# A conv-attention hybrid on one core: a warm start from one half with ten steps, new orders of issue, and the last group of a recurrence stored plainly

## Chip, core and metric

The kernel runs on one core of one Trainium2 chip. The metric is the device time of one execution in microseconds, the median of several runs. The profile is of one further execution. The engines are called as in the profile: PE is TensorE's matmuls, PEld its weight loads, DVE VectorE, ACT ScalarE, POOL GpSimd, SP SyncE.

## What is computed

The input is x of 4 x 128 x 64 x 64 (batch, channels, rows, columns), in fp32. Layer 0 is a layer norm over channels, a depthwise 3x3 convolution added to it, and attention inside 16 x 16 windows with a 5 x 5 neighbourhood (two branches, four heads), added to x. Layer 1 works on the 4096 tokens of each image: a causal linear attention, and then a feed-forward part that ends in a serial recurrence:

```python
t = t + _L1_attn_ref(_ln_t(t), L1_attn_W, L1_attn_b)      # elu features, cumulative sums
t = t + _L1_ffn_ref(_ln_t(t), L1_ffn_W, L1_ffn_V, L1_ffn_gamma, L1_ffn_beta)

# inside _L1_ffn_ref: Wx is batch-normed over all 4 x 4096 tokens
def step(yt, wx_t):
    yt = jax.nn.sigmoid(wx_t + yt @ Vt)
    return (yt, yt)
y0 = jnp.zeros((B, H), dtype=Wx.dtype)
_, ys = jax.lax.scan(step, y0, jnp.swapaxes(Wx, 0, 1))
```

V is orthogonal and the sigmoid's slope is at most a quarter, so the recurrence forgets its start quickly.

## The kernel before

**Main stage.** The 64 rows of an image are cut into four bands of 16, a band into four windows; there are 16 bands and 64 windows. For each band `front()` yields layer norm and convolution in small pieces (`norm_rows`, `convolve`, L314-418: measure, scale, turn, then nine taps, the first on ScalarE, eight on VectorE at L378). For each window `block()` does q, k, v (L427, L440), logits and their exponentials (L480, L489), `sums` (L509, the denominators, copied to `den` and sent by DMA to `dc`), `values` (L524), `inverse` (L535 and L537 on VectorE, then a DMA to `rd` and one from there into `rden`) and `scaled` (L552, on POOL, into oT). When the four windows of a band have their oT, layer 1 does the band in two halves, called a and c (or y and z when the next band is already there): output (L578, 585), measure, norm, turn, queries, keys, values, turn_keys, scores, accumulate, attend0, attend1, measure_last, keep, send, spread, product. product (L726) multiplies by W of the feed-forward part into `wx` and takes the batch norm's statistics of it. send and spread carry the layer norm's factors through DRAM (L609, L620), so that product needs no turned copy; the very last half has none and goes through norm_last and turn_last instead (L730, 731).

**What sets the order.** All engines work in the order of the program; `in_order()` fixes it. The order is written out by hand: `SLOT` is that of a window in the loop, with six gaps (0 to 5); `LAYER1` fills the 24 gaps of a band's four windows with layer 1's operations, `AHEAD` with pieces of `front()`. `START` is the order of everything before the loop's first window (window 4), `TAIL` that of everything after the logits of window 63. `prepare` (L201) folds weights together once. `mul.2` and `mul.3` do the convolution of windows 2 and 3 of the first band on TensorE (nine taps of two matmuls each, four taps at the first call and five at the second, L396); `conv.0` and `conv.1` do windows 0 and 1 on VectorE. `warm.n` asks for n filler matmuls (L259) before the next matmul group; they compute nothing that is used.

**Recurrence.** An image's 4096 steps are cut into 128 segments of 32, run side by side: 512 columns in three groups (L931). Every segment is first run for WARM = 11 steps from zero over the last 11 steps of its segment; the end state is handed to the next segment as its start (L1007), and then 32 counted rounds run. In each round TensorE adds V·y to seeded sums (L1004; VectorE writes the seeds of two rounds at a time, L942) and ScalarE takes the sigmoid (L1009). Outputs of images 0 and 1: four rounds fill a buffer `ys` (three of them), and a DMA on POOL's queue adds it to what `keep` put into the output before (L1016, accumulating). Outputs of images 2 and 3: the residual was parked by `keep`, is loaded into `res` (L913), and POOL adds it round by round into `ot` (L1022), which SP sends (L1028). At the end VectorE compares the 32nd state of every segment with the handed state (L1035), within 5e-7; if any differs by more, `general()` computes everything again with the plain serial recurrence.

Of the kernel before, what the change touches and what calls it, by code (L numbers as in the profile page):

```python
# [9 lines left out]
F32 = mybir.dt.float32  # L10
# [7 lines left out]
P = 128  # L18
# [20 lines left out]
WARM = 11  # L39
# [4 lines left out]
    "measure_last.z",  # L44
# [3 lines left out]
    "norm.a",  # L48
    "measure.c keep.z",
    "",  # L50
    "turn.a norm.c",
    "",
    "",
    "keys.a product.z",
    "turn.c queries.a",
    "values.a",
    "turn_keys.a scores.a keys.c",
    "accumulate.a values.c",
    "turn_keys.c attend0.a queries.c",
    "attend1.a",  # L60
    "scores.c",
    "measure_last.a",
    "accumulate.c keep.a send.a",
# [3 lines left out]
    "",  # L67
)
SLOT = ("sums", "values", "logits", 0, "scaled", "inverse", 1, "q", 2, 3, "k", "v", 4, 5)
AHEAD = ("03", "01223345", "001245", "00234")  # L70
START = (
    "warm.5 conv.0 prepare q.0 front conv.1 mul.2 mul.3",
    "mul.2 k.0 front v.0 q.1 k.1 logits.0 front",
    "q.2 front front front front mul.3 v.1 front",
    "logits.1 sums.0 k.2 values.0 v.2 front front front",
    "inverse.0 front front load.2 front logits.2 q.3 front",
    "front sums.1 scaled.0 front values.1 inverse.1 q.4 k.4",
    "sums.2 k.3 front front front v.3 scaled.1 logits.3",
    "values.2 v.4 inverse.2 front front",
)  # L80
TAIL = (
    "scaled.61 keep.w output.y send.w sums.63 spread.w output.z measure.z",
    "measure.y inverse.62 norm.z values.63 product.w norm.y turn.y scaled.62",
    "keys.y queries.y scores.y turn_keys.y inverse.63 turn.z values.z values.y",
    "queries.z keys.z accumulate.y warm.1 attend0.y turn_keys.z product.v attend1.y",
    "measure_last.y scores.z accumulate.z send.y spread.y attend0.z attend1.z keep.y",
    "measure_last.z warm.2 send.z scaled.63 product.y warm.10 output.a measure.a",
    "output.c measure.c norm.a spread.z keep.z turn.a norm.c turn.c",
    "queries.a queries.c keys.a values.a keys.c turn_keys.a values.c scores.a",
    "accumulate.a attend0.a attend1.a scores.c turn_keys.c measure_last.a accumulate.c keep.a",  # L90
    "attend0.c send.a attend1.c measure_last.c spread.a keep.c norm_last.c product.a",
    "turn_last.c product.z product.c",
# [20 lines left out]
def conv_attn_hybrid(ctx: ExitStack, tc: tile.TileContext, ins: dict, out: bass.AP):  # L113
# [120 lines left out]
    wx = const.tile([P, B, NH, SEG, HSEGS], F32, name="wx")  # L234

# [490 lines left out]
    def product(h):  # L726

        wps = bank()
        if h.factors is None:
            nc.tensor.matmul(wps, fwT, h.xl, start=True, stop=True)  # L730
            nc.scalar.copy(wx[:, h.b, h.hb], wps.rearrange("p (k s) -> p s k", s=SEG))
        else:
            nc.tensor.matmul(wps, fwT, h.rs.rearrange("p s k -> p (s k)"), start=True, stop=True)  # L733
            nc.vector.tensor_tensor(
                wx[:, h.b, h.hb].rearrange("p s (j a) -> p s j a", a=P // SEG),
                wps.rearrange("p (s j a) -> p s j a", j=4, a=P // SEG),
                h.factors.rearrange("p (a s) j -> p s j a", s=SEG),
                ALU.mult,
            )
# [147 lines left out]
    which.update(a=Half(len(bands) - 1, 0), c=Half(len(bands) - 1, 1))  # L887
    for what in " ".join(TAIL).split():
        if what.partition(".")[2].isdigit():
            block(what)  # L890
        else:
            do(what, which)
# [11 lines left out]
    ring = rec.enter_context(tc.tile_pool(name="ring", bufs=3))  # L904
# [4 lines left out]
    res = sp.tile([P, B // 2, NH, SEG, HSEGS], F32, name="res")  # L909
    for s0 in (0, SEG // 2):  # L910
        steps_of, cols = slice(s0, s0 + SEG // 2), slice(s0 * HSEGS, (s0 + SEG // 2) * HSEGS)
        for i, b in enumerate(resd):
            (nc.sync, nc.scalar)[i].dma_start(  # L913
                res[:, i, :, steps_of].rearrange("p n s k -> p n (s k)"), resd[b][:, :, cols]
            )


    mv = sp.tile([P, 2], F32, name="mv")
    nc.vector.bn_aggr(mv, stats.rearrange("p n s -> p (n s)"))
    sc = sp.tile([P, 1], F32, name="sc")  # L920
    nc.gpsimd.tensor_scalar(sc, mv[:, 1:2], 1e-5, 1.0, ALU.add, ALU.mult)
    nc.gpsimd.tensor_tensor(sc, sc, mhalf[:, :1], ALU.pow)
    nc.vector.tensor_tensor(sc, sc, gamma, ALU.mult)
    shift = sp.tile([P, 1], F32, name="shift")
    nc.vector.tensor_tensor(shift, mv[:, 0:1], sc, ALU.mult)
    nc.vector.tensor_tensor(shift, beta, shift, ALU.subtract)


    rounds = [(s, False) for s in range(SEG - WARM + 1, SEG)] + [(s, True) for s in range(SEG)]
    COLS = B * SEGS  # L930
# [4 lines left out]
    def seed(k, g):  # L935


        if 2 * k < len(rounds):
            s, (m0, m1) = rounds[2 * k][0], GROUPS[g]
# [3 lines left out]
                seeds[k, g].rearrange("p r (m k) -> p r m k", k=HSEGS),  # L943
                wxm[:, s : s + 2, m0:m1, :],
# [16 lines left out]
    for t in (mv[:, :1], sc, shift):  # L961
# [21 lines left out]
    for m0, m1 in GROUPS:  # L983
        nc.scalar.activation(
            ys[:, m0:m1, s % RUN, :], wxm[:, s, m0:m1, :], AF.Sigmoid, bias=shift, scale=sc
# [4 lines left out]
    for r, (s, counts) in enumerate(rounds):  # L990
        for g in (0, 1) if r % 2 == 0 else (2,):
            seed(r // 2 + 1, g)
# [4 lines left out]
        for g, (m0, m1) in enumerate(GROUPS):  # L997
            z = seeds[r // 2, g][:, r % 2, :]
# [15 lines left out]
        if counts:  # L1014
            if s % RUN == RUN - 1:
# [4 lines left out]
                )  # L1020
            ot = ring.tile([P, COLS // 2], F32, tag="ot", name="ot", bufs=8)
            (nc.vector if s == SEG - 1 else nc.gpsimd).tensor_tensor(  # L1022
# [711 lines left out]
```

## Time and profile before

| what | us |
|---|---|
| median of 3 runs (838.75 to 840.38) | 839.15 |
| profiled execution, its own time | 843.62 |
| its span, first to last instruction | 841.8 |
| first q of window 0 on TensorE | 18.71 |
| output of band 0's layer 1 on TensorE begins | 72.00 |
| output.a of band 15 begins | 746.85 |
| first sigmoid of the recurrence | 784.08 |
| first sigmoid of round s=0 | 795.66 |
| last sigmoid ends | 828.41 |
| flag ready (`bad`) | 831.44 |

A row of the order of time gives start, duration, engine, line, operation, what it writes and reads (names of the program), shapes and how many; in brackets how long the engine was idle before it and what ended that. A row of the busy time by stage gives the stretch, its length, the busy time of each engine with the number of instructions, the granted TensorE clock as a share of full speed, the mean share of the 16 DMA engines in use, and GB/s.

### The profile page before, as it was taken

The page shows a single profiled execution, that of the slowest core. Times are in us where ns is not written, and L with a number is a line of the kernel's source. Part 1 is how long each engine was busy: PE and PEld are TensorE (multiplying, and loading weights), DVE is VectorE, ACT ScalarE, POOL GpSimd, SP SyncE. Part 2 cuts the span into 40 slices and gives each one's busy share as a digit, 9 for nine tenths or more (in the row PEclk, how much of TensorE's full clock was granted, in tenths as well). Part 3 has the DMA queues.
Part 4 walks back from the last instruction along what each step waited for, and adds up shares of the span by engine and source line. Part 5 has one row for each costly group of instructions (what it writes and reads, how often), then busy time and mean ns, then how long its engine had stood idle before and what let it go on. Part 6 is the DMA issues. An engine that isn't in the chain of part 4 may idle for free.

```text
span 841.8 us, 28915 instructions
## 1 busy us (share of the span) xinstructions
PE 806.6 (96%) x11803; PEld 642.3 (76%) x11805; DVE 693.2 (82%) x2127; ACT 530.8 (63%) x1026; POOL 254.2 (30%) x365
## 2 busy tenths in 40 slices
PE   6998999999999999999999999999999999988993
PEld 3766787878787878778787878787878878756792
DVE  6565989897989998998989898998999886466882
ACT  3675757676757576666767676757666665613782
POOL 2122232423233232413142323323332303121193
PEclk7999999999999999999999999999999999999997
DMA  4022141332323231414132232323141313121697
GB/s 140 18 64 70 42 113 42 79 79 66 91 68 97 57 103 36 109 42 119 40 86 75 62 87 67 96 65 98 39 108 39 92 41 95 44 56 38 209 224 174
DMA packets 81422, 68.81 MB, mean 82 GB/s; under 512 B 44800, under 2 KB 63872, under 8 KB 81280
## 3 DMA queue, kind: packets, MB, share of 16 engines
q1 hardware_dynamic: 53200, 43.47, 18.0%
q10 hardware_dynamic: 26928, 19.20, 9.2%
q0 software_dynamic: 1152, 4.19, 2.9%
q8 instruction: 95, 1.56, 0.8%
q14 instruction: 47, 0.39, 0.2%
HBM read 39.51 MB, written 17.89 MB: 68 GB/s over the span
## 4 chain that ended last, share of the span: by engine, by line
PE 86%; DVE 4%; DMA 4%; POOL 2%; ACT 1%; issue 1%; ACTq 0%; DVEq 0%; POOLq 0%; SPq 0%
PE bank L427 12%; PE bank L509 7%; PE bank L480 7%; PE bank L625 7%; PE bank L578 7%; PE bank L524 6%; PE bank L440 6%; PE bank L302 5%; PE bank L641 4%; PE z L1004 4%; PE bank L679 3%; PE bank L662 3%; PE bank L698 3%; PE bank L700 3%; PE bank L733 3%; PE bank L467 2%
## 5 line engine op out<-in xcount | busy, mean ns | idle before, releaser
L378 DVE SCALAR_TENSOR_TENSOR y<-ypad,cpe_w,y 128x512 f32<-128x512 f32 x240 | 191.7, 799 | 12.7 <-ACT y L376 7.7
L489 ACT ACTIVATE es<-bank 128x512 f32<-128x512 f32 x256 | 132.2, 604 | 32.1 <-PE bank L480 31.7
L285 POOL TENSOR_SCALAR rs<-mv 128x4 f32<-128x4 f32 (+2 forms) x100 | 25.3, 253 | 390.8 <-DVE mv L283 389.1
L552 POOL TENSOR_TENSOR oT<-o_sb,rden 128x512 f32<-128x512 f32 x64 | 83.0, 1297 | 119.1 <-DMA rden<-rd 104.2
L286 POOL TENSOR_TENSOR rs<-rs,mhalf 128x4 f32<-128x4 f32 (+2 forms) x100 | 106.0, 1060 | 8.3
L524 PEld LDWEIGHTS bank<-es,v_sb 128*32 128x32 f32 x3072 | 62.9, 110 | 39.2 <-issue 21.3
L480 PEld LDWEIGHTS bank<-q,k 32*64 32x64 f32 x4096 | 75.4, 130 | 2.7
L480 PE MATMUL bank<-q,k 32*64 32x96 f32 (+1 forms) x4096 | 77.5, 274 | 0.0
L512 ACT COPY den<-bank 128x512 f32<-128x512 f32 x64 | 37.4, 584 | 55.8 <-PE bank L509 55.3
L524 PE MATMUL bank<-es,v_sb 128*32 128x96 f32 (+1 forms) x3072 | 69.5, 237 | 1.6 <-DMA v_sb<-v_sb 1.6
L578 PEld LDWEIGHTS bank<-woT,oT 128*128 128x128 f32 x512 | 61.0, 196 | 13.2 <-POOL oT L552 9.6
L509 PE MATMUL bank<-es,ones 128*32 128x512 f32 x512 | 69.6, 605 | 0.6 <-ACT es L489 0.6
L427 PE MATMUL bank<-y2w,wqT 128*128 128x256 f32 x256 | 67.4, 386 | 2.4 <-DVE y2w L378 2.2
L625 PE MATMUL bank<-xl,awT 128*128 128x512 f32 x128 | 66.6, 607 | 0.0
L578 PE MATMUL bank<-woT,oT 128*128 128x128 f32 x512 | 62.3, 281 | 4.5 <-POOL oT L552 4.5
L427 PE MATMUL bank<-y2w,wkT 128*128 128x256 f32 x256 | 65.9, 380 | 0.0
L440 PE MATMUL bank<-wvT,y2w 128*128 128x256 f32 x256 | 65.9, 380 | 0.0
L535 DVE TENSOR_TENSOR dc<-dc,pad_c 128x32 f32<-128x32 f32 x64 | 25.5, 399 | 47.8 <-DMA dc<-den 47.7
L435 ACT COPY k<-bank 128x512 f32<-128x512 f32 x64 | 38.6, 603 | 41.2 <-PE bank L427 41.2
L627 ACT ACTIVATE low<-bank,minus 128x512 f32<-128x512 f32 x64 | 43.8, 685 | 24.5 <-PE bank L625 23.4
L427 PEld LDWEIGHTS bank<-y2w,wkT 128*128 128x128 f32 x256 | 47.3, 190 | 13.4 <-issue 7.5
L629 DVE SCALAR_TENSOR_TENSOR f<-low,bank 128x512 f32<-128x512 f32 x64 | 43.5, 680 | 16.6 <-ACT low L627 16.6
(131 smaller groups left out, 1687.9 us busy)
## 6 DMA issues: line engine op xcount, KB each, us to landing
rden<-rd SPq DMA_DIRECT2D x64, 256.0 KB
v_sb<-v_sb SPq DMA_DIRECT2D x128, 64.0 KB
factors<-factors ACTq DMA_DIRECT2D x31, 256.0 KB
xin<-in_xt SPq DMA_DIRECT2D x15, 512.0 KB
out<-rs_o ACTq DMA_DIRECT2D x16, 256.0 KB
resd<-rs_o ACTq DMA_DIRECT2D x16, 256.0 KB
out<-ot SPq DMA_DIRECT2D x32, 128.0 KB
out<-ys POOLq DMA_DIRECT2D x8, 512.0 KB, 7.4
```

Source lines behind the costliest of these rows:

```text
L286: nc.gpsimd.tensor_tensor(rs[:, :n], rs[:, :n], mhalf[:, :n], ALU.pow)
L378: nc.vector.scalar_tensor_tensor(y2, src, cpe_w[:, tap : tap + 1], y2, ALU.mult, ALU.add)
L427: nc.tensor.matmul(pps[:, br * WT : (br + 1) * WT], wT[:, br * P : (br + 1) * P], y2, start=True, stop=True,)
L440: nc.tensor.matmul(vps[:, e * 256 : (e + 1) * 256], y2[:, e * P : (e + 1) * P], wvT, start=True, stop=True,)
L480: nc.tensor.matmul(sps[h][half * KC : (half + 1) * KC, cols], w["k"][rows, k0 : k0 + KC], w["q"][rows, cols], start=False, stop=br == BR - ...
L489: nc.scalar.activation(es, sps[h], AF.Exp, scale=scale)
L509: nc.tensor.matmul(dps[rows], ones[:, :HD], w["es", h], start=True, stop=True)
L524: nc.tensor.matmul(ops[rows, cols], w["v"][:, n, c0 : c0 + HD], w["es", h][:, cols], start=(br, n) == pieces[0], stop=(br, n) == pieces[-1],)
L552: nc.gpsimd.tensor_tensor(oTs[n][:, :, :, wj * WS : (wj + 1) * WS], w["o"].rearrange("p (a r c) -> p a r c", a=BR, c=WS), w["rden"].rearra ...
L578: nc.tensor.matmul(yps[:, j * P : (j + 1) * P], oT[:, br, t], woT[:, br, :], start=br == 0, stop=br == BR - 1,)
L625: nc.tensor.matmul(zps, awT[:, m * P : (m + 1) * P], h.xl, start=True, stop=True)
L627: nc.scalar.activation(low, zps, AF.Exp, bias=minus)
```

## The change

- WARM goes from 11 to 10. The warm run starts from y = 0.5 in every channel: V times 0.5 is added to beta once (`beta0`), and the first sigmoid of the warm run uses a shift with it (`shift0`).
- The order lists LAYER1, the third entry of AHEAD, START and TAIL are new.
- In the last half, product takes its statistics from PSUM, aggregates at once, has POOL begin the scale, and VectorE instead of ScalarE copies wx out.
- The ys ring has four buffers. The last group of four rounds of images 0 and 1 is not accumulated by DMA: its residual is loaded into `end_a` early, VectorE adds round by round, and ScalarE's queue stores it plainly. The last `ot` is added by POOL like the others.
- The number of rounds is now odd (41), so the seed pairs start one round off.

```diff
-WARM = 11
+WARM = 10
+GUESS = 0.5
 LAYER1 = (
-    "measure_last.z",
+    "",
     "",
     "product.y send.z output.a",
     "measure.a spread.z output.c",
-    "norm.a",
-    "measure.c keep.z",
-    "",
-    "turn.a norm.c",
+    "keep.z norm.a",
+    "measure.c",
+    "turn.a",
+    "norm.c",
     "",
     "",
-    "keys.a product.z",
-    "turn.c queries.a",
-    "values.a",
-    "turn_keys.a scores.a keys.c",
-    "accumulate.a values.c",
-    "turn_keys.c attend0.a queries.c",
-    "attend1.a",
+    "queries.a values.a turn.c",
+    "product.z keys.a",
+    "turn_keys.a",
+    "scores.a keys.c queries.c accumulate.a",
+    "values.c",
+    "turn_keys.c attend0.a attend1.a",
+    "",
     "scores.c",
-    "measure_last.a",
-    "accumulate.c keep.a send.a",
+    "measure_last.a keep.a",
+    "accumulate.c send.a",
     "",
     "",
     "attend0.c spread.a attend1.c",
-    "",
+    "measure_last.c",
 )
-AHEAD = ("03", "01223345", "001245", "00234")
+AHEAD = ("03", "01223345", "001455", "00234")
 START = (
-    "warm.5 conv.0 prepare q.0 front conv.1 mul.2 mul.3",
-    "mul.2 k.0 front v.0 q.1 k.1 logits.0 front",
-    "q.2 front front front front mul.3 v.1 front",
-    "logits.1 sums.0 k.2 values.0 v.2 front front front",
-    "inverse.0 front front load.2 front logits.2 q.3 front",
-    "front sums.1 scaled.0 front values.1 inverse.1 q.4 k.4",
-    "sums.2 k.3 front front front v.3 scaled.1 logits.3",
-    "values.2 v.4 inverse.2 front front",
+    "prepare conv.0 front warm.3 mul.2 conv.1 mul.3 q.0",
+    "k.0 front front mul.2 v.0 q.1 k.1 front",
+    "logits.0 q.2 front front mul.3 front front v.1",
+    "sums.0 logits.1 front values.0 front front front k.2",
+    "inverse.0 scaled.0 v.2 front front load.2 front logits.2",
+    "front sums.1 front values.1 q.3 warm.6 sums.2 inverse.1",
+    "q.4 k.3 v.3 warm.2 front logits.3 scaled.1 front",
+    "values.2 inverse.2 front k.4 front v.4 front",
 )
 TAIL = (
...
-    "measure_last.y scores.z accumulate.z send.y spread.y attend0.z attend1.z keep.y",
-    "measure_last.z warm.2 send.z scaled.63 product.y warm.10 output.a measure.a",
-    "output.c measure.c norm.a spread.z keep.z turn.a norm.c turn.c",
...
-    "attend0.c send.a attend1.c measure_last.c spread.a keep.c norm_last.c product.a",
-    "turn_last.c product.z product.c",
+    "warm.2 warm.4 output.y keep.w send.w scaled.61 spread.w sums.63",
...
+    "attend1.y measure_last.y send.y product.v scaled.63 warm.3 spread.y accumulate.z",
+    "keep.y scores.z attend0.z attend1.z measure_last.z output.a send.z measure.a",
+    "product.y output.c measure.c norm.a turn.a keep.z norm.c values.a",
...
+    "spread.a keep.c norm_last.c product.a product.z turn_last.c product.c",
 )
...
         if h.factors is None:
             nc.tensor.matmul(wps, fwT, h.xl, start=True, stop=True)
-            nc.scalar.copy(wx[:, h.b, h.hb], wps.rearrange("p (k s) -> p s k", s=SEG))
+            nc.vector.bn_stats(stats[:, h.b * NH + h.hb, :], wps)
+            nc.vector.bn_aggr(mv, stats.rearrange("p n s -> p (n s)"))
+            nc.gpsimd.tensor_scalar(sc, mv[:, 1:2], 1e-5, 1.0, ALU.add, ALU.mult)
+            nc.gpsimd.tensor_tensor(sc, sc, mhalf[:, :1], ALU.pow)
+            nc.vector.tensor_scalar(shift, mv[:, 0:1], -1.0, None, ALU.mult)
+            nc.vector.tensor_copy(wx[:, h.b, h.hb], wps.rearrange("p (k s) -> p s k", s=SEG))
+            return
...
+    v0 = bank()[:, :1]
+    nc.tensor.matmul(v0, fvT, guess, start=True, stop=True)
+    nc.vector.tensor_tensor(beta0, beta, v0, ALU.add)
     for what in " ".join(TAIL).split():
...
-    ring = rec.enter_context(tc.tile_pool(name="ring", bufs=3))
+    ring = rec.enter_context(tc.tile_pool(name="ring", bufs=4))
...
+    nc.sync.dma_start(
+        end_a.rearrange("p m r k -> p (m r k)"),
+        out_a[SEG // RUN - 1].rearrange("p m r k -> p (m r k)"),
+    )
...
     nc.vector.tensor_tensor(sc, sc, gamma, ALU.mult)
-    shift = sp.tile([P, 1], F32, name="shift")
-    nc.vector.tensor_tensor(shift, mv[:, 0:1], sc, ALU.mult)
-    nc.vector.tensor_tensor(shift, beta, shift, ALU.subtract)
+    nc.vector.scalar_tensor_tensor(shift0, shift, sc, beta0, ALU.mult, ALU.add)
+    nc.vector.scalar_tensor_tensor(shift, shift, sc, beta, ALU.mult, ALU.add)
...
         if counts:
-            if s % RUN == RUN - 1:
+            if s >= SEG - RUN:
+                nc.vector.tensor_tensor(
+                    end_a[:, :, s % RUN], end_a[:, :, s % RUN], last[:, :NA], ALU.add
+                )
+            elif s % RUN == RUN - 1:
                 nc.gpsimd.dma_start(
                     out_a[s // RUN].rearrange("p m r k -> p (m r k)"),
                     ys[:, :NA].rearrange("p m r k -> p (m r k)"),
                     accum_op=ALU.add,
                 )
+            if s == SEG - 1:
+                nc.scalar.dma_start(
+                    out_a[s // RUN].rearrange("p m r k -> p (m r k)"),
+                    end_a.rearrange("p m r k -> p (m r k)"),
+                )
             ot = ring.tile([P, COLS // 2], F32, tag="ot", name="ot", bufs=8)
-            (nc.vector if s == SEG - 1 else nc.gpsimd).tensor_tensor(
+            nc.gpsimd.tensor_tensor(
```

## The prediction

> **What bounds the kernel now.** I read the page's shares and its 40 slices first, then the busy time by stage, then the order of time where a stage shows idle TensorE, then the DMA rows.
>
> ```profile
> PE 806.6 (96%) x11803; PEld 642.3 (76%) x11805; DVE 693.2 (82%) x2127; ACT 530.8 (63%) x1026; POOL 254.2 (30%) x365
> ...
> PEclk7999999999999999999999999999999999999997
> ```
>
> TensorE is busy 96% and at full clock but for the two ends. By stage (columns: stretch, its length, busy us of PE, PEld, DVE, ACT, POOL with counts, granted clock, DMA share, GB/s):
>
> ```profile
> 14.00:18.00 4.00, 2.53 (x6) 1.35 (x4) 3.26 (x7) 0.49 (x1) 0.04 (x1) 0.50 0.06 19
> ...
> 56.00:60.00 4.00, 2.63 (x125) 2.14 (x117) 3.93 (x13) 1.16 (x4) 1.28 (x2) 1.00 0.15 40
> 66.00:72.00 6.00, 2.59 (x43) 1.81 (x29) 1.33 (x6) 4.16 (x8) 1.31 (x2) 1.00 0.30 82
> 72.00:78.00 6.00, 6.00 (x36) 5.92 (x37) 2.88 (x12) 0.81 (x1) 1.25 (x5) 0.72 0.15 46
> 370.00:415.00 45.00, 45.00 (x715) 36.37 (x715) 39.54 (x128) 30.02 (x56) 14.03 (x19) 1.00 0.31 77
> ```
>
> The middle has nothing to give: a band takes 45 us, all of them TensorE's (100 to 640 us: 0.5 us idle). The start has: 1.4 us idle in 56-60, 3.4 in 66-72, and half clock (14-18, and part of 72-78). The close of the main stage, in order of time (start, us, engine, line, what; in brackets what the engine waited for):
>
> ```profile
> 744.22 2.34 PE L259 MATMUL bank<-zeros 128*128 128x512 bf16 x10
> ...
> 744.56 1.01 POOL L286 TENSOR_TENSOR rs<-rs,mhalf 128x4 f32<-128x4 f32 x1
> 745.54 1.26 POOL L552 TENSOR_TENSOR oT<-o_sb,rden 128x512 f32<-128x512 f32 x1
> 746.85 3.84 PE L578 MATMUL bank<-woT,oT 128*128 128x128 f32 x32 [0.30 <-POOL oT L552]
> 747.43 1.04 DVE L734 TENSOR_TENSOR wx<-bank,factors 128x512 f32<-128x512 f32 x1 [3.24 <-DMA factors<-factors]
> ```
>
> Ten filler matmuls hide a wait: output.a (L578) needs scaled.63 (L552), which stands on POOL behind the power of measure_last.z (L286). The recurrence, by stage as above:
>
> ```profile
> 785.50:795.00 9.50, 9.50 (x58) 8.59 (x59) 8.70 (x16) 8.37 (x30) 0.00 (x0) 1.00 1.00 320
> 795.00:806.00 11.00, 11.00 (x74) 10.25 (x72) 9.48 (x17) 9.77 (x37) 8.37 (x12) 1.00 0.55 124
> 816.00:822.00 6.00, 6.00 (x38) 5.47 (x38) 5.19 (x11) 5.28 (x19) 5.73 (x10) 1.00 1.05 241
> ...
> 829.00:832.00 3.00, 0.23 (x2) 0.09 (x2) 2.05 (x9) 0.00 (x0) 1.15 (x2) 0.75 1.11 267
> 832.00:835.00 3.00, 0.00 (x0) 0.00 (x0) 0.00 (x0) 0.00 (x0) 0.00 (x0) 0.50 1.02 206
> ```
>
> The DMA share is full from about 802 to 836, long after the last sigmoid (828.4): the outputs, not the rounds, set the end. The page's queue and issue rows give the price of the accumulating store:
>
> ```profile
> q0 software_dynamic: 1152, 4.19, 2.9%
> ```
>
> 2.9% of 841.8 us is 24.4 us of all engines for eight, 3.05 us each; four rounds (3.9 us) bring one of these and four stores of ot, so a backlog grows. One more row, of ScalarE:
>
> ```profile
> 824.62 0.72 ACT L1009 ACTIVATE ys<-z 128x176 f32<-128x176 f32 x3 [1.33 <-DMA out<-ys]
> ```
>
> This stall (three ys buffers, a store not yet landed) is a consequence of the backlog.
>
> **The change part by part.** Gains are against the profiled execution: span 841.8, itself 843.62 us, 4.5 above the median 839.15; I take them off the median.
>
> *Start: 6.0 us.* I place the new order by hand with the trace's durations, up to window 6's k (77.2 now, behind output.a and output.c). From q.0 (18.71) to there TensorE lost 5.2 us idle, 1.4 to half clock up to 21.5, and 1.7 in 72.7-76.2: 8.3. The new order puts `prepare` at about 12.5 and 16 of the 36 tap matmuls of windows 2 and 3 before q.0. VectorE does prepare's six operations (2.0 us) before conv.0, so q.0 slips from 18.7 to some 20.5 (+1.8); the 16 matmuls at 0.216 us are then behind (-3.5); eight fillers after q.0 cost 8 x 0.21 (+1.7). These cancel. What remains is how much of the 8.3 goes. Window 3's oT decides: now its `den` is copied at 59.4 only (ScalarE waited 2.85 us for VectorE's convolution), its sum lands at 64.3, oT is ready at 71.95. In the new order the second turn of band 1 comes some 3 us earlier, VectorE starts that convolution at about 34.3 instead of 37.3, `sums.k` are asked for earlier than `inverse.k`, and oT is ready at about 66, where TensorE would be at 64: about 2 us of stall stay. 8.3 - 2.0 = 6.3; I take 6.0. Bounds: 8.3 (nothing left), 1.4 (only the first clock window won).
> Here the Trainium skill bears on the sum (*TensorE: Matmul & The Clock Gate*, Part 1): full clock returns after one busy window of some 3.4 us, and idle ones take it away. The row agrees for the loss (0.50 in 14-18, 0.56 in 18-22). By the rule TensorE, busy from 12.5 on, is at full speed by about 18, as I assumed; if it stays halved to 21.5 as in the row, the 16 tap matmuls cost twice, 3.5 more, and the start gives 2.5.
>
> *LAYER1 and AHEAD: 0.* The same instructions, in other gaps. TensorE has no idle time to win there (at most the 1.2 us between 100 and 730). What hides the new order is slack: keys.a now stands in the last gap before a window's sums, turn_keys.a right after its logits, 3.5 us of TensorE work later; the other operations have one gap more or less. Bounds: -1 to +3.
>
> *Tail: 3.0 us.* scaled.63 now stands before accumulate.z. Its rden was issued at 734.4 and takes 3.9 us (for the window before: 727.3 to 731.2), so it is there at 738.3; behind measure_last.y on POOL (to 740.8) it ends at 742.05. TensorE is through with the attends of z and keep.y at 742.5; with three fillers output.a starts at about 743.0, 3.8 us earlier. Not all of it passes: product.y now stands between measure.a and output.c on VectorE and waits for factors that land at 747.4; then 1.04 + 0.69 + 0.65 + 1.2 gives norm.a at 751.0 against 752.66: 1.7. product.z (1.9 us at half clock in front of product.c) moves ahead of turn_last; VectorE's queue then ends at 780.24 against 780.74: 0.5. Of the 1.7 us lost to half clock in 755.4-758.8 I count half. Bounds 1 to 4.3. v0 (a one-column matmul, 0.2 us, and an add of 0.16) and the six fillers lie in the 0.55 us wait for es before sums.63 or cost 0.2.
>
> *Batch norm's end: 0.2.* From bn_stats to the first sigmoid now: 780.74 to 784.08, 3.34. New: stats from the bank 0.69 (no such row; SBUF 0.69, an add reading a bank 0.65: 0.55 to 0.85), aggregate 1.02, POOL 0.19 + 0.56, two VectorE steps of 0.16 instead of three, six handovers of some 0.06: 3.14. The copy of wx moves from ScalarE (0.58) to VectorE (0.7 to 1.03, the row of L734 with the same write), under POOL's 0.98: up to 0.25 sticks out.
>
> *One round less: 0.97* (the seed pairs are 1.94 apart). The ring's fourth buffer alone: 0, since the stores wait for DMA anyway.
>
> *The plain end: 1.4.* The last accumulation (3.05) becomes a load of 512 KB, in the half idle stretch 795-806, and a plain store: at the 320 GB/s of 785-795, 0.524 MB take 1.64. The four adds on VectorE (128x256, rows of 0.41 to 0.93) have behind them the seeds of two rounds later, with 1.5 us to spare; the last replaces ot's 0.93. The store stands last on ScalarE's queue; SP's queue gets one issue (0.4) before its 32 ot, 12 us early. The skill (*DMA: Bandwidth & Descriptors*, Anatomy of one DMA) prices a DMA at about 2.0 us plus bytes over 436 GB/s, 3.2 here as an estimate: by it the store, issued about 0.9 after the last sigmoid, would not be last; by the row the backlog of some 7.9 us (828.4 to 836.3) decides. I take the row.
>
> Sum: 6.0 + 0 + 3.0 + 0.2 + 0.97 + 1.4 = 11.6. 839.15 - 11.6 = **827.5**; the profiled one at 832.0.
>
> **The rivals.**
> - *The start's wait comes back.* If window 3's oT is as late as now, other work only moves around the stall: 1.4 for the start, 7.0 in all, 832.2. For it: four DMAs in a row (den, rd, rden, each 2 to 4 us) are in no order's power.
> - *DMA stops being the end.* With four buffers and a plain store the queue drains before the flag's branch (now 833.4, 3 us ahead of the DMA end); then the end wins 2.1 more: 825.4. Against: 35 us of transfers in 34 us of rounds.
> - *Slower: keys to turn_keys.* VectorE runs 88% full in a band; its row for this f ends
>
> ```profile
> 270.80 0.67 DVE L629 SCALAR_TENSOR_TENSOR f<-low,bank 128x512 f32<-128x512 f32 x1
> ```
>
>   at 271.5, with turn_keys.a due at 272.2: 0.7 us of slack. If VectorE lags by 1.8 more, TensorE waits 1.1 us in each of 15 bands, 16.5: 844. It decides above 0.8 us a band. Against: VectorE idles 4.5 us a band and TensorE's order stays.
> - *The guess doesn't hold.* Ten steps from 0.5 must end within 5e-7 of the run from the true start, or the general path runs. On the reference's inputs in single precision I get 2.4e-7 (eleven from zero: 2.1e-7), so a margin of two. Else some 4096 serial steps of 0.6 us (z 0.31, sigmoid 0.32) come on top: over 3,000 us.
>
> **How the numbers follow.** The forecast 0.50; the start's wait 0.30; DMA not the end 0.13; within 0.2% 0.02; keys 0.04; the guess 0.01. A change of 0.2% is about what a measurement of this kernel can tell from none. Range: 821.5 (start 8.3, tail 4, end 2.1 more, less what can't hold at once) to 834.0 (start 1.4, tail 1.5). Faster 0.93, same 0.02, slower 0.05.
>
> **What would show it.** Start: window 6's k at about 71 instead of 77.2, no idle of 3.4 before L578. Middle: a band still 45.0; more is the keys rival. Tail: output.a right after fillers, the first sigmoid some 9.2 earlier than 784.08. End: 9 rounds before s=0, no ACT wait for out<-ys, DMA share full to the last landing, 7 us past the last sigmoid. I am wrong if the start shows the same oT wait, or if the end moves by more than the start of the stores did.

## The result and the profile after

The changed kernel takes 834.87 us (median of 8 runs, 832.40 to 837.44) where the kernel before takes 841.12 beside it (median of 8, 838.75 to 844.43): a ratio of 0.992, 95% interval 0.9902 to 0.9939, 6.3 us less. Two more sets gave 0.9923 (0.9896 to 0.9951) and 0.993 (0.9905 to 0.9954). These ratios are not the quotients of the two medians, which give 0.9926 here and 0.9903 and 0.9926 in the other sets. The forecast was 827.5, a gain of 11.6, with a range of 821.5 to 834.0: faster, as said, but by about half, and 0.9 us above the range. Of the 7.4 us between forecast and time, 2.0 lie in the kernel before, whose median was 839.15 in the three runs that the forecast starts from.

The profiled run took 832.40 us (span 830.7), 11.2 less than the profiled run of before. Of this only 6.3 is the kernel's: the profile of before was one of its longer runs, that of after the shortest of its eight. That its 832.40 us come so near the 832.0 forecast for a profiled execution is luck. The page of the profile after, its shares, its clock and the queue of the accumulating stores:

```profile
PE 799.6 (96%) x11802; PEld 640.5 (77%) x11808; DVE 691.8 (83%) x2134; ACT 530.3 (64%) x1022; POOL 254.7 (31%) x365
...
PEclk9999999999999999999999999999999999999897
...
q0 software_dynamic: 1008, 3.67, 2.5%
```

One accumulation fewer (2.5% of 830.7 us, seven of them, 2.97 each), and full clock except near both ends. By stage, with the columns of before:

```profile
60.00:66.00 6.00, 3.46 (x83) 2.89 (x65) 0.77 (x3) 4.94 (x10) 1.80 (x4) 1.00 0.29 82
66.00:70.00 4.00, 4.00 (x35) 3.90 (x33) 2.97 (x13) 0.41 (x1) 0.41 (x3) 1.00 0.06 10
...
767.00:771.50 4.50, 0.03 (x1) 0.00 (x1) 4.34 (x7) 1.49 (x2) 0.77 (x3) 0.88 0.29 80
771.50:777.40 5.90, 5.90 (x15) 3.41 (x16) 3.38 (x9) 1.37 (x3) 0.09 (x1) 0.51 1.03 348
...
797.00:812.00 15.00, 15.00 (x93) 13.60 (x92) 12.94 (x24) 13.25 (x48) 13.48 (x21) 1.00 1.06 245
...
822.00:825.00 3.00, 0.00 (x0) 0.00 (x0) 0.00 (x0) 0.00 (x0) 0.00 (x0) 0.50 0.87 321
```

The start keeps 2.5 us of idle TensorE in 60-66 and, in this profile, no half clock behind it (66-70 shows 1.00). The end is DMA's as before: its share is 1.06 in 797-812 and still 0.87 in 822-825, and the last output lands at 825.2, 7.0 us behind the last sigmoid. New are the two rows in the middle: TensorE stands still for 4.5 us, then works 5.9 us at half clock. In order of time, all engines, rows of other operations left out:

```profile
764.60 1.12 PE L738 MATMUL bank<-xl,fwT 128*128 128x512 f32 x2 [0.68 <-ACT xl L624]
...
765.61 1.02 DVE L748 TENSOR_TENSOR wx<-bank,factors 128x512 f32<-128x512 f32 x1 [2.06 <-DMA factors<-factors]
765.78 1.25 PE L267 MATMUL bank<-zeros 128*128 128x512 bf16 x5
...
768.92 0.68 DVE L739 BATCH_NORM_STATS2 stats<-bank 128x6 f32<-128x512 f32 x1
769.64 1.02 DVE L740 BATCH_NORM_AGGREGATE mv<-stats 128x2 f32<-128x192 f32 x1
...
770.76 0.68 DVE L744 COPY wx<-bank 128x512 f32<-128x512 f32 x1
...
771.50 2.74 PE L267 MATMUL z<-zeros 128*128 128x512 bf16 x6 [4.47 <-DVE wx L744]
...
772.07 1.37 ACT L1002 ACTIVATE ys<-wx,shift,sc 128x176 f32<-128x176 f32 x3 [0.61 <-DVE shift L941]
...
777.36 8.82 PE L1025 MATMUL z<-ys,fvT 128*128 128x176 f32 x54
```

The same place in the kernel before:

```profile
780.12 0.58 ACT L731 COPY wx<-bank 128x512 f32<-128x512 f32 x1 [2.18 <-PE bank L730]
...
781.45 1.48 PE L259 MATMUL z<-zeros 128*128 128x512 bf16 x6
...
784.08 1.37 ACT L984 ACTIVATE ys<-wx,shift,sc 128x176 f32<-128x176 f32 x3 [0.79 <-DVE shift L926]
...
784.95 1.08 PE L1004 MATMUL z<-ys,fvT 128*128 128x176 f32 x4
```

The recurrence's PSUM banks are those of the main stage, the last product's among them. Before, ScalarE emptied that bank at once, and TensorE ran on through the fillers of the new banks (z<-zeros) and the products of mv, sc and shift: 0.87 us from the first sigmoid to the recurrence's first product. Now the last product (L738) is in its bank at 765.72, but VectorE empties it, at 770.76: on VectorE the copy stands behind two other halves' multiplications by their factors (wx<-bank,factors; the first waits for its factors until 765.61) with their statistics, and then behind this bank's own statistics, the aggregate and the shift. TensorE's queue stands behind that copy, its clock falls to 0.51, and the first product comes 5.29 us after the first sigmoid. The first sigmoid is 12.0 us earlier than before, the first product 7.6.

### The profile page after: what moved, and what is told of

Same layout as the page of the kernel before. It is cut to its first block, busy times and chain, and to the rows that moved or that the text cites. A ratio compares the mean times of both kernels' runs of the same rounds, so it can differ in the third digit from the quotient of the medians.

```text
span 830.7 us, 28903 instructions
## 1 busy us (share of the span) xinstructions
PE 799.6 (96%) x11802; PEld 640.5 (77%) x11808; DVE 691.8 (83%) x2134; ACT 530.3 (64%) x1022; POOL 254.7 (31%) x365
## 4 chain that ended last, share of the span: by engine, by line
PE 90%; DVE 4%; DMA 3%; POOL 1%; ACT 1%; issue 1%; ACTq 0%; DVEq 0%; SPq 0%; POOLq 0%
PE bank L435 13%; PE bank L488 8%; PE bank L517 7%; PE bank L633 7%; PE bank L586 6%; PE bank L532 6%; PE bank L448 6%; PE bank L310 6%; PE z L1025 5%; PE bank L649 4%; PE bank L670 3%; PE bank L706 3%; PE bank L687 3%; PE bank L708 3%; PE bank L747 3%; PE bank L475 3%
## 5 line engine op out<-in xcount | busy, mean ns | idle before, releaser
L386 DVE SCALAR_TENSOR_TENSOR y<-ypad,cpe_w,y 128x512 f32<-128x512 f32 x240 | 185.4, 773 | 16.5 <-ACT y L384 12.0
L488 PE MATMUL bank<-q,k 32*64 32x160 f32 (+1 forms) x4096 | 77.5, 274 | 0.0
L633 PE MATMUL bank<-xl,awT 128*128 128x512 f32 x128 | 63.1, 593 | 0.1
L586 PE MATMUL bank<-woT,oT 128*128 128x128 f32 x512 | 60.4, 275 | 2.5 <-POOL oT L560 2.5
L443 ACT COPY q<-bank 128x512 f32<-128x512 f32 x64 | 38.7, 605 | 27.3 <-PE bank L435 21.1
L289 DVE BATCH_NORM_STATS2 st<-x 128x6 f32<-128x128 f32 x256 | 55.4, 279 | 0.6
```

Of the source, the lines that this page charges most:

```text
L386: nc.vector.scalar_tensor_tensor(y2, src, cpe_w[:, tap : tap + 1], y2, ALU.mult, ALU.add)
L443: nc.scalar.copy(w[name], pps)
L488: nc.tensor.matmul(sps[h][half * KC : (half + 1) * KC, cols], w["k"][rows, k0 : k0 + KC], w["q"][rows, cols], start=False, stop=br == BR - ...
L586: nc.tensor.matmul(yps[:, j * P : (j + 1) * P], oT[:, br, t], woT[:, br, :], start=br == 0, stop=br == BR - 1,)
L633: nc.tensor.matmul(zps, awT[:, m * P : (m + 1) * P], h.xl, start=True, stop=True)
```

## The experiments

**My theory after the two profiles**: the gains before that place and behind it are there, and the copy's move takes some 4 us of them back. **The rival**: the profile pair misleads, a forecast gain (start, tail or end) is missing in the time, and the late copy costs nothing in the time. The first runs undo one part at a time, or mend the copy. Each time stands beside runs of the kernel before on the same chip.

**copy_act: ScalarE empties the bank**

```diff
-            nc.vector.bn_stats(stats[:, h.b * NH + h.hb, :], wps)
+            nc.scalar.copy(wx[:, h.b, h.hb], wps.rearrange("p (k s) -> p s k", s=SEG))
+            nc.vector.bn_stats(stats[:, h.b * NH + h.hb, :], wx[:, h.b, h.hb].rearrange("p s k -> p (s k)"))
...
-            nc.vector.tensor_copy(wx[:, h.b, h.hb], wps.rearrange("p (k s) -> p s k", s=SEG))
```

> The changed kernel, but in the last half ScalarE copies the product out of PSUM at once, as before the change, and the statistics are taken from that copy. Theory 1 (the bank): the fillers that open the recurrence's banks waited 4.5 us for VectorE's late copy, TensorE's clock fell to half and the recurrence's first matmul came 5.3 us after the first sigmoid's start instead of 0.9; with the copy on ScalarE the fillers start right after the product, the first matmul follows the first sigmoid's start by about 1 us, and the time falls by 3 to 4.5 us against the changed kernel: ratio to before about 0.988. Theory 2 (one unlucky execution: the late fillers cost nothing in most): same as the changed kernel, 0.992.

0.9904 (0.9875 to 0.9934), and in a second set, as copy_act_again:

> ScalarE's copy alone, once more, since its first 6 times (0.9875 to 0.9934) leave open whether it is worth 0 or 4 us. Theory: at full clock a held bank costs 1.6 us of which the seeds take back 0.8, with half clock behind it 4.4 less 0.8; whether half clock comes depends on where the 3.41 us stretches fall, so 0.8 to 3.6 us, on the mean some 2: 0.9895. Rival (the seeds take back all): 0.992. In the profile the first product is 0.9 us behind the first sigmoid in either.

0.988 (0.9856 to 0.9905). The order of time of the first of the two:

```profile
770.83 0.58 ACT L739 COPY wx<-bank 128x512 f32<-128x512 f32 x1 [1.22 <-PE bank L738]
...
772.63 1.47 PE L267 MATMUL z<-zeros 128*128 128x512 bf16 x6 [0.54 <-DVE wx L750]
...
776.27 1.37 ACT L1004 ACTIVATE ys<-wx,shift,sc 128x176 f32<-128x176 f32 x3 [0.59 <-DVE shift L943]
...
777.16 9.01 PE L1027 MATMUL z<-ys,fvT 128*128 128x176 f32 x50
```

The fillers wait 0.54 us and for another copy, the clock stays full, and the first product is 0.89 us behind the first sigmoid (776.27). That the statistics are taken from the copy changes nothing else: from their start to the first sigmoid it takes 3.14 us, 3.15 in the changed kernel. The mean of the two ratios is 0.9892, that of the changed kernel's three 0.9924: the late copy costs 0.0032, 2.7 us, in the time, give or take 2.0 by the intervals.

**Parts of the change undone**: start_old and tail_old take START or TAIL of the kernel before, layer1_old LAYER1 with AHEAD, and end_old the accumulating store for the last four steps (with the last `ot` on VectorE, as before).

```diff
-START = (
-    "prepare conv.0 front warm.3 mul.2 conv.1 mul.3 q.0",
...
+START = (
+    "warm.5 conv.0 prepare q.0 front conv.1 mul.2 mul.3",
...
```

> The changed kernel with the old START. By the two profiles the new START brought window 6's k 8.2 us earlier, so theory 1 expects the time 6 to 8 us longer than the changed kernel's, a ratio to before of 1.000. Theory 2 (the start's gain is mostly taken back later, or is not there in most executions) expects 2 us or less, 0.994.

0.9977 (0.9963 to 0.9992): the new start is worth 0.0047 to 0.0057 of the time (against the three ratios of the changed kernel), 4.0 to 4.8 us, less than the 6 to 8 that the profiles of the pair suggested. The wait of before is back in its profile; the changed kernel's row stands below it:

```profile
72.41 5.46 PE L586 MATMUL bank<-woT,oT 128*128 128x128 f32 x32 [3.31 <-POOL oT L560]
```

```profile
65.46 1.72 PE L586 MATMUL bank<-woT,oT 128*128 128x128 f32 x13 [2.54 <-POOL oT L560]
```

```diff
-TAIL = (
-    "warm.2 warm.4 output.y keep.w send.w scaled.61 spread.w sums.63",
...
+TAIL = (
+    "scaled.61 keep.w output.y send.w sums.63 spread.w output.z measure.z",
...
```

> The changed kernel with the old TAIL (product.z again between turn_last and product.c). By the profiles the new TAIL brings output.a of band 15 some 4 us earlier, but the first sigmoid only 1.6 us (12.0 less the 10.4 at the last logits). Theory 1: 1 to 2 us longer than the changed kernel, 0.994. Rival: the old order keeps TensorE busier in front of the recurrence, the clock stays up, and the time is the same or shorter, 0.990 to 0.992.

0.9906 (0.9877 to 0.9935): with the old order the kernel is not slower at all. The rival has it: beside the late copy the new tail gains nothing in the time. With the old order TensorE idles 1.95 us before the recurrence's fillers instead of 4.47, and its first product comes 60.6 us behind the last logits, where the three profiles of the changed kernel have 62.9 to 63.4.

```diff
...
-AHEAD = ("03", "01223345", "001455", "00234")
+AHEAD = ("03", "01223345", "001245", "00234")
```

> The changed kernel with the order LAYER1 and AHEAD of before. Theory: the new order is worth what the two profiles differ by from output band 1 to output band 14 (588.64 against 585.87 us: 2.8 us, of it 1.1 in waits for oT): then 0.995 of the kernel before. Rival (my forecast): the order of LAYER1 is worth nothing, and the 2.8 us are half-clock stretches and jitter of single executions: 0.992, and the stretch from output band 1 to band 14 is 586 us with the old order too.

0.9924 (0.9894 to 0.9953), the changed kernel in the same set 0.9923. The stretch from output band 1 to 14 is 587.66 us, between the two expectations (588.64 and 586). That is 1.8 us more than in the three profiles of the changed kernel (585.8 to 585.9), but late_store below, with the new order, has 587.30, so a single profile can't tell. The time shows nothing, with an interval of 0.3%.

```diff
-            if s >= SEG - RUN:
...
-            elif s % RUN == RUN - 1:
+            if s % RUN == RUN - 1:
...
```

> The changed kernel, with the last group of rounds accumulated by DMA like the others and the last ot added by VectorE, as before; the ring keeps its four buffers. If the DMA backlog sets the end, the time is longer by 3.05 - 1.64 = 1.4 us than the changed kernel's, 0.9935. If the flag's path sets the end, nothing changes, 0.992.

0.9951 (0.9935 to 0.9966): the plain end is worth 0.0021 to 0.0031, 1.8 to 2.6 us. In its profile the last transfer lands 8.4 us behind the last sigmoid, in the three of the changed kernel 6.3 to 7.3.

**warm11: eleven rounds from one half**

```diff
-WARM = 10
+WARM = 11
```

> The changed kernel with eleven warm rounds, begun from one half as its ten are. From the recurrence's first product to its last sigmoid 41.80 us where the changed kernel takes 40.83 in both profiles (a round is 0.97 us), the time 0.97 us more: 0.9935. Rival (a round hides in the transfers that end the kernel): 0.992. So small a difference the times can't tell apart, the stretch in the profile can.

0.9909 (0.9893 to 0.9925), which can't tell; from the first product to the last sigmoid 41.76 us against 40.83: a round is 0.93 us. The last transfer lands 6.9 us behind the last sigmoid, as in the changed kernel (6.3 to 7.3), so the profile shows none of it hidden.

**fill_more: is it the clock or the queue?** TensorE does products of zeros through the wait for the bank.

```diff
-    fill(bank(), 6)
+    fill(bank(), 24)
```

> The changed kernel with 24 instead of 6 products of zeros behind the last product (18 more of 0.217 us: 3.9 us, inside TensorE's wait of 4.4 us for VectorE's copy of wx). They compute nothing that is used. Theory: of the 5.3 us from the first sigmoid to the recurrence's first product 2.5 us are the work queued behind the bank (12 to 14 products at full clock, as in two other runs) and 2.8 us come from the half clock that TensorE's idle time brings; with TensorE busy the clock stays up, and 2.5 us are left: 0.989 to 0.9905 where the changed kernel is 0.992. Rival: the half clock there belongs to the stretch before the idle time, or comes whether TensorE is busy with zeros or not: 5.3 us again, 0.992.

0.9901 (0.9881 to 0.9921). The order of time:

```profile
765.66 5.39 PE L267 MATMUL bank<-zeros 128*128 128x512 bf16 x24
...
771.11 1.46 PE L267 MATMUL z<-zeros 128*128 128x512 bf16 x6
...
771.36 1.38 ACT L1002 ACTIVATE ys<-wx,shift,sc 128x176 f32<-128x176 f32 x3 [0.59 <-DVE shift L941]
...
774.15 8.82 PE L1025 MATMUL z<-ys,fvT 128*128 128x176 f32 x54
```

The bank is just as late, but the fillers take 1.46 us and not 2.74, and the first product is 2.79 us behind the first sigmoid instead of 5.29. So 1.6 to 1.9 us are the queue behind the bank (2.5 to 2.8 against 0.9), the other 2.5 the half clock that the idle time brings. The other profiles in which TensorE waits for the late copy show the same steps, and they go by how long it idles before the fillers: after 0.8 to 2.0 us (four profiles) there is no half clock over the queue and the first product is 2.49 us behind the first sigmoid; after 2.7 to 4.0 (four) there is one stretch of 3.41 us and it is 4.0 to 4.2; after 4.4 and 4.5 there are two and it is 5.4 and 5.3.

**The tail's missing gain.** In the order of time above VectorE waits 2.06 us for the factors of the last band's first half before it can begin the batch norm's last pieces. Their way is a 2 KB store (SyncE) and a load (ScalarE). After, then before:

```profile
757.45 0.33 ACTq L727 DMA_DIRECT2D resd<-rs_o  x1
757.62 0.32 SPq L617 DMA_DIRECT2D factors<-rs  x1
...
761.91 0.33 ACTq L628 DMA_DIRECT2D factors<-factors  x1
```

```profile
770.87 0.32 SPq L609 DMA_DIRECT2D factors<-rs  x1
771.01 0.33 ACTq L719 DMA_DIRECT2D resd<-rs_o  x1
772.27 0.33 ACTq L620 DMA_DIRECT2D factors<-factors  x1
```

The load goes out 4.29 us after the 2 KB store where the 256 KB store went out ahead of it, 1.40 where it followed. late_store issues the 256 KB store behind the load, copy_store does so with ScalarE's copy; send_first and copy_send put it on SyncE's queue behind the 2 KB store instead.

```diff
             nc.scalar.dma_start(h.factors, h.sent.unsqueeze(0).to_broadcast([P, P, 4]))
+            if getattr(h, "late", False):
+                nc.scalar.dma_start(resd[h.b][:, h.hb], h.rs.rearrange("p s k -> p (s k)"))
...
         if h.b in resd:
+            if h.n == len(bands) - 1 and h.s == 0:
+                h.late = True
+                return
```

> The changed kernel, but the 256 KB store of the last band's first half (resd<-rs_o) is issued behind the load of its factors instead of 0.17 us ahead of the 2 KB store that this load waits for. Theory: the 2 KB store took 4.25 us because it went out beside the 256 KB store (1.40 us in the kernel before, where it went out 0.14 us ahead of it), and VectorE's wait for the factors (2.06 us) holds the whole end of the batch norm. Then that store takes 1.4 us, VectorE's wait is gone, and the time is 1.2 to 2.1 us less: 0.9895 to 0.9905 of the kernel before where the changed kernel is 0.992. Rival: the wait of VectorE is covered by TensorE's last product and the copy behind it anyway; then 0.992, the wait for the factors gone and another in its place.

> Both mends together: ScalarE copies the last product out of its PSUM bank at once (the statistics are then taken from the copy), and the 256 KB store is issued behind the load of the factors. Theory (the two waits stand one behind the other on the path): 1.6 to 4.4 us for the bank (the first product of the recurrence 0.9 us behind the first sigmoid instead of 2.5 to 5.3) and 1.2 to 2.1 us for the factors: 2.8 to 6.5 us less than the changed kernel, 0.984 to 0.9885 of the kernel before. Rival (they lie beside each other, or TensorE's products of the last band come next): no better than either alone, 0.9895 to 0.991.

0.9914 (0.9883 to 0.9945) and 0.9903 (0.9866 to 0.9939). VectorE's wait for the factors is 0.3 us or gone, but from the last logits to the first sigmoid it takes 57.87 and 57.20 us where the changed kernel took 57.66 and 57.75 (and 59.27 in its third profile). Another wait stands in its place in late_store: ScalarE's copy of the second half waits until 767.43 for the store that now lands late. The rival holds. The theory of the 2 KB store fails too: with no large store beside it, it still takes 2.8 us in both, not 1.4.

```diff
         nc.sync.dma_start(h.sent, h.found2[2])
+        if getattr(h, "late", False):
+            nc.sync.dma_start(resd[h.b][:, h.hb], h.rs.rearrange("p s k -> p (s k)"))
...
```

> The changed kernel, but the 256 KB store of the last band's first half goes out on SyncE's queue right behind the 2 KB store of its scale factors, instead of on ScalarE's queue 0.17 us ahead of it. Theory: the 2 KB store then takes about 1.4 us and not 4.3, VectorE's wait for the factors (1.2 to 2.1 us) is gone, and, since the store is not held back as it was in the run that issued it behind the load of the factors, ScalarE's copy of the second half is not held either: the first sigmoid 1.2 to 2.1 us nearer to the last logits (57.7 us in both profiles of the changed kernel), 0.9895 to 0.991 of the kernel before. Rival: another wait stands in its place; 57.2 us or more, 0.992.

> ScalarE copies the last product out of its PSUM bank at once, and the store goes out on SyncE's queue behind the factors. Theory: from the last logits to the recurrence's first product 56.5 us (55.6 to the first sigmoid and 0.9 behind it) where the changed kernel took 63.0 and 63.1; at full clock the recurrence takes back 0.8 us of what it is given, since it then waits for VectorE's seeds: 2.5 to 5 us less than the changed kernel, 0.986 to 0.989 of the kernel before. Rival: TensorE's own products of the last band end last then, and no more than the copy's share is gained: 0.9895 to 0.991.

0.9898 (0.9879 to 0.9916) and 0.9863 (0.9846 to 0.988). The first sigmoid is 57.51 and 57.21 us behind the last logits, and 56.30 in a repeat of copy_send (below): the expected 55.6 is missed. Against the changed kernel's first two profiles that is 0.2 to 1.5 us, no more than its own three differ by. The 2 KB store still takes 2.9 and 3.1 us, more than the 1.4 expected.

**copy_tail: what the new order is worth with the bank free**: copy_act with TAIL of before.

> The changed kernel with ScalarE's copy of the last product and the order TAIL of before. It settles what the new order of the tail is worth when the PSUM bank is not held. Theory (the new order shortens the way to the first sigmoid by 0.6 to 1.6 us in the profiles, and the held bank is what it lost them to): from the last logits to the recurrence's first product 59.1 us (58.2 and 0.9), where the changed order with the same copy took 58.3; 0.991 to 0.992 of the kernel before, the new order with the same copy 0.9904. Rival (the new order is worth my 3.0 us once the bank is free): 0.9935 to 0.995.

0.9881 (0.9853 to 0.991), copy_act_again in the same set 0.988: faster than either expectation. The profiles give the new order 57.4 and 57.9 us from the last logits to the first sigmoid, the old one 58.26; the times give it nothing, though an interval of some 3 us between the two does not exclude a part of it.

**norm_only, norm_copy_send: the new wait inside the tail**

```diff
-    "product.y output.c measure.c norm.a turn.a keep.z norm.c values.a",
+    "output.c norm.a product.y measure.c turn.a keep.z norm.c values.a",
```

> The changed kernel with one step of TAIL moved: output.c and norm.a ahead of product.y instead of behind it and measure.c. Theory: TensorE idles 3.16 us before turn.a because norm.a stands on VectorE behind product.y and its statistics (1.7 us) and output.c with measure.c (1.85 us), though its factor is there 2.0 us earlier, and half clock follows (3.41 us, 1.7 lost); with norm.a ahead the wait is 1.2 us or less and the time 1.5 to 3.6 us less: 0.988 to 0.990. Rival (the end of the batch norm is set by the factors and the held bank, whatever TensorE does before): 57.7 us from the last logits to the first sigmoid again, 0.992.

> ScalarE's copy, the store behind the factors on SyncE's queue, and norm.a ahead of product.y. Theory: the three gains add up, 54.5 to 56 us from the last logits to the first sigmoid where copy and store alone took 57.2, and 0.9 to the first product: 0.982 to 0.985 of the kernel before. Rival: the factors' way (last attends, measure, two DMAs) ends last whatever comes before: 57.2 us, 0.986.

0.9922 (0.9892 to 0.9951) and 0.9877 (0.985 to 0.9903). TensorE's wait before turn.a, in the changed kernel and in norm_only:

```profile
739.98 1.24 PE L310 MATMUL bank<-ident,xn 128*128 128x128 f32 x4 [3.16 <-DVE xn L301]
```

```profile
738.15 1.10 PE L310 MATMUL bank<-ident,xn 128*128 128x128 f32 x4 [1.25 <-DVE xn L301]
```

The first sigmoid comes 56.09 and 55.41 us behind the last logits, less than in any profile without the step (56.30 the least). In norm_only TensorE also idles only 1.8 us before the fillers, and the first product is 2.49 us behind the first sigmoid: 58.6 us behind the last logits, where the changed kernel has 62.9 to 63.4. The times do not show it: both kernels are where they would be without the step, by the ratios. This stays open; with six runs each the intervals would hide 2 us, and the quotient of norm_only's two medians is 0.990, not 0.992.

**The pair side by side**

> The changed kernel once more, so that the others of this set have it beside them. 0.992 of the kernel before, about 834.5 us. If single runs differ by 2.5 us because the half-clock stretches of 3.41 us fall elsewhere in each, then this profile has TensorE's wait for VectorE's copy of wx again (4.5 us where it is followed by half clock or not) and the wait of VectorE for the factors again (1.2 to 2.1 us before the product of the last band's first half), but its half-clock stretches elsewhere than in the first profile, and the stretch from the first sigmoid to the recurrence's first product between 2.5 us (full clock) and 5.3 us (half clock). If instead that stretch belongs to the kernel's order, it is 5.3 us again.

> The changed kernel beside its mended version, on one chip. 0.992 of the kernel before. If the half-clock stretches that follow TensorE's idle time fall where a grid of 3.41 us, not tied to the kernel's start, puts them, then a profile that begins at another place of the grid than the first two (their stretches began at 2.4 and 2.6 us of it) has the first product 2.5 to 5.4 us behind the first sigmoid and window 6's k up to 4 us later; if it begins at the same place, 5.3 and 69 again.

> ScalarE's copy and the store behind the factors once more. If both mends stand in the time: 0.986 to 0.988 of the kernel before and 3.5 to 5 us under the changed kernel of the same set. If the first 0.9863 was a lucky set of times: 0.989 to 0.990. The first product 0.9 us behind the first sigmoid in either case.

after_again gave 0.9923 and the first profile almost to the tenth (5.38 us to the first product). after_third gave 0.993, with 4.16 us: of its two half-clock stretches near the end (768.3 and 775.1, 3.41 us each) only the second lies over the queue behind the bank. Beside it copy_send_again gave 0.9877 (0.9855 to 0.99), 831.93 us against 835.05. So the mended kernel beats both: 0.9863 and 0.9877 of the kernel before, 0.987 on the mean where the changed one has 0.9924, 4.5 us less.

## Why the prediction was wrong, by its own steps

**Batch norm's end: the step whose mechanism failed.** It said "The copy of wx moves from ScalarE (0.58) to VectorE", "under POOL's 0.98: up to 0.25 sticks out", and counted 0.2 us to the good. As VectorE's time that is right: from the last statistics' start to the first sigmoid it took 3.15 us where the step had 3.14. What it left out is who else waits for that bank, and so put TensorE's wait at nothing. The copy is also the release of a PSUM bank; fourteen matmuls, the recurrence's fillers first, are queued between that release and the first product. Shown in the profiles of copy_act and fill_more: 1.6 us of queue and up to 2.8 of half clock, of which the recurrence takes 0.8 back (with the bank free, VectorE writes 13 seeds without a pause from 776.60 in copy_act while the rounds already run, and they take 41.6 us instead of 40.83); 2.7 us in the times, give or take 2.0. In place of +0.2 the term is -2.7.

**Tail: 3.0, mis-sized by as much.** It is 0 in the times within some 0.3% (tail_old, copy_tail). The mechanism of its first part was right: output.a starts 17.8 us behind the last logits instead of 22.1, and norm.a begins 2.7 us sooner by the same count. But TensorE then idles 3.16 us before turn.a, since norm.a stands behind product.y and measure.c on VectorE, and at the far end VectorE waits for factors. Of 3.0 us some 1.6 reach the first sigmoid in the profile pair, but nothing in the changed kernel's third profile (59.27 us from the last logits, 59.28 in the kernel before); 0.4 to 0.8 reach it between the kernels with ScalarE's copy, and none is seen in the times. The two terms are not independent: with the old tail TensorE idles less at the held bank, so that the late copy costs less there (2.49 us to the first product, against 4.2 to 5.4). What swallows the rest is not shown; with the one wait shortened (send_first) the time is 2.2 us lower, with the other (norm_only) 0.2, each with an interval of about 2 us, and send_first also had no half clock over the queue.

**Start: 6.0, right in kind.** "About 2 us of stall stay": 2.54 did. "Window 6's k at about 71": in the 18 profiles with the new START it stands at 68.9 to 73.9, 71.4 on the mean, where the old one had 77.31 and 77.71. So k comes 6.1 us sooner on the mean, but the time gives 4.0 to 4.8; what takes the rest is not shown. The row and the skill's rule were weighed for the half clock of the start: TensorE has full clock from 16.1 on in the profiled run, and from 15.0 to 18.2 on in the 18, as the sum assumed by the rule.

**LAYER1 0, one round 0.97, the plain end 1.4**: 0.0; 0.93; 1.8 to 2.6 by the times and 1.1 to 2.1 by the landings. The DMA backlog decided, as the row said. The skill's price, which its section states for the DMAs that POOL issues, did not fit this store on ScalarE's queue: issued at 819.0, its last packet ended at 824.4, 5.4 us instead of 3.2. Its packets filled all engines for 1.28 us (queue q10, 6.4% of the 20 us from 818 on) where the sum had 1.64 and an accumulation takes 2.97; that alone makes the term 1.7. The load of `end_a` was issued at 769.7, not in 795-806.

**The sum**: 4.4 + 0 + 0 - 2.7 + 0.9 + 2.2 = 4.8, where 6.3 was measured (5.1 to 8.2 by its interval); each measured term has an interval of some 2 us of its own, so they agree. Against the forecast the batch norm's end is short by 2.9, the tail by 3.0 and the start by 1.6, and the plain end is 0.8 over. The range's lower end, 821.5, is also less than its own terms allow: with start 8.3, tail 4 and the end's 2.1 more the sum is 822.2. Without the late copy the change gives 0.9892, 9.1 us, 832.0 beside 841.12, inside the forecast's range. Of the rivals, "the start's wait comes back" forecast a gain (7.0) near the one measured, but its mechanism was not the cause; none of the rivals was.

## What to carry to other kernels

A copy out of PSUM is two things, data for its reader and a bank for its next writer: before moving it to another engine or behind other work, ask who writes that bank next and what is queued behind that write. When TensorE gets ahead of the chain that ends a stage, its lead turns into idle time, and here idle time, 2.7 us of it or more, into half clock for the next stage's first products: it has to be filled or avoided. Single profiles of this kernel differ by more than most of its edits are worth; a part's worth is read from the times of kernels that differ by that part alone, and the profile tells why.

## What was not expected of the hardware

Half clock comes in stretches of 3.41 us or 6.83 (10.24 at the start of the kernel before), and where they fall differs between runs of one kernel. Within a run all of them, the one behind the last work too, begin whole multiples of 3.41 us apart: in the changed kernel's first profile at 12.67, 739.71 and 770.43, 213 and 9 multiples. In the 18 profiles with the new START, window 6's k stands at 68.9 to 70.6 us where no such stretch begins between 65.9 and 68.9 us (seven profiles), 71.0 to 73.3 with one of 3.41 (seven), and 73.5 to 73.9 with one of 6.83 (four): the later k goes with the stretch, by 1.7 to 2.4 us for each 3.41, and at the end, by the steps from 2.5 to 5.4, it was some 1.5. The Trainium skill (*TensorE: Matmul & The Clock Gate*, Part 1) says that the window is free-running and the half-clock time thus varies by run; these profiles agree and give it a price of up to 5 us at this place, as much as the eight runs of the changed kernel spread (5.0). That it is the same spread is likely, not shown: over the 80 runs of the kernel before on record with the experiments, time and granted clock go together with a correlation of -0.78.

With a 256 KB store issued 0.17 us ahead, a 2 KB store let the load behind it go after 3.4 to 4.5 us in ten profiles and after 2.1 in one (start_old). With that store 0.4 us behind it, it took 2.8 to 3.1 us (four profiles), with none near it 2.8 (late_store, copy_store), and 1.4 in the three profiles with the old TAIL, where the large store followed 0.14 us behind on another queue. So the store ahead explains a part of the 4.3 us; what makes 2.8 and 1.4 differ is open.
